# Sixteen transposes of a batch in one group, and an earlier carry, from the seventh batch on

## The chip, the cores and the metric

The kernel runs on one core of a Trainium2 chip. The core has five engines with an instruction queue each: TensorE (PE; PEld is its weight load, which overlaps the matmuls), VectorE (DVE), ScalarE (ACT), GpSimd (POOL), and SyncE (SP), which here only issues DMAs. An engine takes its queue in order, and the engines meet at semaphores. The metric is the device time of one execution in microseconds (us), lower is better; a time is the median of several runs.

## The reference

Sixteen batches of 512 tokens with 512 features each. One layer, in two halves:

```
# half 1: h = rmsnorm(layernorm(x)) * g_res @ W_in.T + b_in
#         p = rmsnorm(ctx)[..., :512] * g_init, scanned over the 512 patches: s[t] = a*s[t-1] + b*p[t]
#         plug = index of the patch of each token, from the running count of boundaries
x = x + s[plug] + h
# half 2 (z = layernorm(x)), z_prev = z shifted by one token
xr = mu_r * z + (1 - mu_r) * z_prev ;  xk = mu_k * z + (1 - mu_k) * z_prev
r  = sigmoid(xr @ W_r.T) ;  k = square(relu(xk @ W_k.T))
x  = x + r * (k @ W_v.T)
```

Everything is in float32. The four products (a: `W_in`, k: `W_k`, r: `W_r`, v: `W_v`) are each a 512x512 by 512x512 product per batch.

## The kernel before, in words

**Products.** Each operand of a product is split into a high and a low part, and a product is high*high + high*low + low*high. A product of a batch is four output tiles of 128x512; a tile is 12 matmuls of 128x512 (3 passes over 4 chunks). So a, k, r and v are 48 matmuls each per batch. In the text, "r tile 2" is the third tile of r; a "row product" is one tile of r or v, whose 128 rows are tokens.

**The stages of a batch b.**
- The context tiles `cx` (four of 128x1024) are loaded by SP; ACT squares them (`junk<-cx`), POOL takes the power (`sq`), DVE scales and chains them (`cx<-cx,sq,bc`, `cx<-cx,cx`: `scan_u`).
- The **carry** (`scan`, lines 744 to 780): three matmuls with a fixed matrix on the high and low parts `ch`, `cl` of the last context tile give `pc`; DVE adds it to the four tiles (`cx<-pc,cx`), SP writes them to a DRAM buffer (`dr<-cx`), and the next context tiles take their room.
- `x` is loaded, its statistics are taken, the bias is added by a POOL DMA (`x<-bc`), and the rows of the scan are added by four **gathers** (`x<-dr,plug`), indirect DMAs of POOL. The index `plug` is made for four batches at a time by small matmuls (`cp`) and DVE work.
- a: four tiles `pa`; `a_end` (`x<-pa,rs,x`, DVE) adds each to x and frees its PSUM tile. It needs the gathers of its rows.
- The second norm (`norm2`: `sb`, `r` on DVE and POOL, `y` on ACT), then the **transposes** (`transp`, lines 848 to 858): four 128x128 transposes for each of the four row tiles, sixteen in all, into the four tiles `tr`.
- `mix` (lines 860 to 878) makes from `tr` the operand `m` of k and of r: ACT (`pv<-tr`), DVE (`pv<-tr,small,pv`), ACT (high part, `m<-pv`), DVE or POOL (low part).
- k: four tiles `pk`; ACT takes relu, square and high part (`kr`, `kr<-kr`, `ka`), DVE or POOL the low part. r: `pr`, then ACT's sigmoid `sg`. v: `pw`, then DVE's `sg<-pw,sg`, and the sum into x, which is stored.

**The order.** A planner (`Plan`, lines 63 to 285) runs a model of the engines on the host while the kernel is built, and gives each engine a fixed order of "pieces" (the row "L300" of the profile is the helper that records every instruction, so groups are told apart by tile names). A piece has a cost, a due time, and a "late" time that is worked backwards from what needs it; `lead` is added to what a piece is held to need. The course of PE is laid out in slots: with i the batch in its second half, a of batch i+1 (as far as not done), k of batch i, then the row products of batch i in the order r0, r1, v0, r2, v1, r3, v2, v3, with the transposes of batch i+1 among them:

```
for k, (w, j) in enumerate((("r", 0), ("r", 1), ("v", 0), ("r", 2), ("v", 1), ("r", 3), ("v", 2), ("v", 3))):
    slot((w, i, j))
    if n1:
        for jj in TAT_OF.get(i, TAT).get(k, ()):
            slot(("t", i + 1, jj), 0.43)
```

`TAT = {0: (0, 1), 2: (2, 3)}` puts eight transposes behind the first row product and eight behind the third; `TAT_OF` has other places for the first batches. The transposes become free to run when the four `y` are there, so the second norm of batch i+1 ends before.

**PSUM tiles.** There are four PSUM tiles of the kind `ps` for pa, pk, pr, pw and pc, and four of the kind `tr`. The planner takes the lowest free one (line 230, `take[k] = (kind, sorted(free[kind])[used])`). In its order most products therefore alternate between two tiles: a product may start only when the engine behind the last product but one has read that one's result. A carry takes a third tile.

**SP.** Each load that takes a buffer also waits for a PE instruction (lines 1268 to 1272), so the loads keep to the planner's order.

Of the kernel before, what the change touches and what calls it, by code (L numbers as in the profile page):

```python
# [316 lines left out]
}  # L317
PASS = 0.935
PERIOD = lambda i: (("a", i + 1), ("k", i))
TAT = {0: (0, 1), 2: (2, 3)}  # L320
TAT_OF = {0: {0: (0, 1, 2, 3)}, 1: {0: (0, 1, 2, 3)}, 2: {0: (0, 1, 2, 3)}}
AHEAD = 20.0
EASE = 1.0
SKIP = 6.0
# [114 lines left out]
NWHOLE = 2  # L439
Y_DVE = (0, 1, 2, 3)  # L440
LEAD = 12.0
HI_DVE = False
U_DVE = True
LOADS = ["raw2"]
# [7 lines left out]
def block_kernel(  # L452
# [59 lines left out]
    def add(engines, fn, r=(), w=(), new=None, **kw):  # L512
        if isinstance(engines[0], str):
            engines = (engines,)
        kinds = {}
        for n, v in (new or {}).items():
            kinds[n], spec[n] = v[0], v[1:]
        kw["stage"] = stage
        if engines is LO and ONLY.get(stage) is not None:
            kw["port"] = (DVE, POOL)  # L520
            engines = (LO[ONLY[stage]],)
        elif engines is HI:
            kw["port"] = (DVE,) if HI_DVE else ()
        elif engines is LO:
            kw["port"] = (DVE, POOL)
        elif engines[0][0] == POOL and "moves" not in kw:
            kw["port"] = (POOL,)
        plan.add(engines, fn, r, w, kinds, **kw)

    def K(name, *parts):  # L530
        return [(name, p) for p in (parts or (0,))]
# [4 lines left out]
    PS = (("ps",), [P, D], F32)  # L536
    PST = (("ps", "tr"), [P, D], F32)
    TRP = (("tr", "ps"), [P, D], F32)
    TR = (("tr",), [P, D], F32)
    HI = ((ACT, 0.52), (DVE, 0.34)) if HI_DVE else ((ACT, 0.52),)  # L540
    LO = ((DVE, 0.61), (POOL, 1.26))
# [202 lines left out]
    def scan(b):  # L744
        def carry(e):
            e.matmul(S[f"pc{b}"], scan_m, S[f"cx{b}_{NJ - 1}"][:, :D], start=True, stop=True)

        if b < NWHOLE:
            add((PE, 1.12), carry, K(f"cx{b}_{NJ - 1}") + K("consts"), K(f"pc{b}"),
                new={f"pc{b}": PST if b == 0 else PS}, lead=LEAD if b > 1 else 0.0)  # L750
        else:
            last, hi, lo = f"cx{b}_{NJ - 1}", f"ch{b}", f"cl{b}"
            TMPR = (("tmp",), [P, D], F32R)
            if b == NWHOLE:
                add((ACT, 0.3), lambda e: e.copy(scan_hi, scan_m), K("consts"), K("scan_r", 0))
                add((DVE, 0.2), lambda e: e.tensor_tensor(scan_lo, scan_m, scan_hi.bitcast(F32), ALU.subtract),
                    K("consts") + K("scan_r", 0), K("scan_r", 1))
            add((ACT, 0.52), lambda e: e.copy(S[hi], S[last][:, :D]), K(last), K(hi), new={hi: TMPR})
            add(LO, lambda e: e.tensor_tensor(S[lo], S[last][:, :D], S[hi].bitcast(F32), ALU.subtract),
                K(last) + K(hi), K(lo), new={lo: TMPR})  # L760

            def carry3(e):
                for i, (w, m) in enumerate(((0, hi), (0, lo), (1, hi))):
                    e.matmul(S[f"pc{b}"], (scan_hi, scan_lo)[w], S[m], start=(i == 0), stop=(i == 2))

            add((PE, 0.72), carry3, K(hi) + K(lo) + K("scan_r", 0, 1), K(f"pc{b}"),
                new={f"pc{b}": PS}, lead=LEAD if b > 1 else 0.0)
        for j in J:
            n = f"cx{b}_{j}"
            add((DVE, 0.6),  # L770
                lambda e, n=n, j=j: e.scalar_tensor_tensor(
                    S[n][:, :D], S[f"pc{b}"], ADEC ** (j + 1), S[n][:, :D], ALU.mult, ALU.add),
                K(f"pc{b}"), K(n))

            def put(e, n=n, j=j):
                if f"dr{b}" not in S:
                    S[f"dr{b}"] = dpool.tile([T, D], F32, tag="dr", name=f"dr{b}")
                e.dma_start(S[f"dr{b}"].rearrange("(p j) d -> p j d", j=NJ)[:, j], S[n][:, :D])

            add((SP, 0.5), put, K(n), K(f"dr{b}", j), moves=0.73)  # L780
# [288 lines left out]
    def slot(key, cost=3 * PASS):  # L1069
        nonlocal t  # L1070
        due[key] = t
        t += cost
# [5 lines left out]
    for i in range(NB):  # L1078
# [5 lines left out]
# [5 lines that stand above are left out]
# [62 lines left out]
    def prepare_batch(b):  # L1151
# [34 lines left out]
        for j in J:  # L1186
            scan_u(b, j, one_go=b == 0 or U_DVE)
        scan(b)
        stage = ("stat1", b)
        for j in J:  # L1190
# [141 lines left out]
```

## Time and profile before

| What | us |
|---|---|
| median of 3 runs | 815.05 |
| lowest and highest run | 812.93, 817.34 |
| the profiled execution, device time | 813.32 |
| its span, from the first to the last instruction | 811.2 |
| PE busy in the span | 789.8 |
| DVE busy | 616.2 |
| ACT busy | 486.7 |
| POOL busy | 449.8 |

The granted clock of PE is 0.997 of full speed over the span. The chain that ended last is PE for 62% of the span, DVE for 12%, DMA for 9%, POOL for 6%, waits on nothing that the profile shows ("issue") 5%, ACT 4%. The three dearest issues of DMA: 64 loads of context tiles (512 KB each, 6.2 us to landing), 64 writes of the scan (256 KB, 3.4 us) and 14 bias additions (1024 KB, 8.1 us).

Busy time of PE is not read as work at its peak: matmuls are pipelined and the profile models their ends. The starts are better. In an undisturbed stretch a row of four 128x512 matmuls begins 0.93 us after the last such row, a tile of twelve takes 2.80 us, and eight transposes 0.79 us.

### The profile page before, as it was taken

The page shows a single profiled execution, that of the slowest core. Times are in us where ns is not written, and L with a number is a line of the kernel's source. Part 1 is how long each engine was busy: PE and PEld are TensorE (multiplying, and loading weights), DVE is VectorE, ACT ScalarE, POOL GpSimd, SP SyncE. Part 2 cuts the span into 40 slices and gives each one's busy share as a digit, 9 for nine tenths or more (in the row PEclk, how much of TensorE's full clock was granted, in tenths as well). Part 3 has the DMA queues.
Part 4 walks back from the last instruction along what each step waited for, and adds up shares of the span by engine and source line. Part 5 has one row for each costly group of instructions (what it writes and reads, how often), then busy time and mean ns, then how long its engine had stood idle before and what let it go on. Part 6 is the DMA issues. An engine that isn't in the chain of part 4 may idle for free.

```text
span 811.2 us, 11218 instructions
## 1 busy us (share of the span) xinstructions
PE 789.8 (97%) x3627; PEld 624.8 (77%) x3627; DVE 616.2 (76%) x1323; ACT 486.7 (60%) x950; POOL 449.8 (55%) x374
## 2 busy tenths in 40 slices
PE   7998999999999999999999999999999999999997
PEld 4776777877777887878787887888778787888885
DVE  6899799989789497686968779685876869784622
ACT  5937496555484566757455775646666564655640
POOL 2843676464675465763647566565665647571300
PEclk9999999999999999999999999999999999999999
DMA  9857486884784773847668392866559477350001
GB/s 321 271 96 263 101 235 175 280 216 131 157 232 131 181 232 74 241 166 198 156 140 242 74 268 107 218 198 184 135 130 246 136 173 216 66 141 2 27 27 52
DMA packets 52554, 134.69 MB, mean 166 GB/s; under 512 B 4752, under 2 KB 5264, under 8 KB 50576
## 3 DMA queue, kind: packets, MB, share of 16 engines
q1 hardware_dynamic: 35744, 102.39, 36.9%
q0 software_dynamic: 16608, 31.46, 23.0%
q8 instruction: 28, 0.46, 0.2%
q14 instruction: 30, 0.25, 0.1%
q10 hardware_dynamic: 144, 0.13, 0.0%
HBM read 85.73 MB, written 33.55 MB: 147 GB/s over the span
## 4 chain that ended last, share of the span: by engine, by line
PE 62%; DVE 12%; DMA 9%; POOL 6%; issue 5%; ACT 4%; SPq 0%; POOLq 0%; DVEq 0%; ACTq 0%
PE pk L300 19%; PE pr L300 15%; PE pw L300 14%; PE pa L300 11%; DMA x<-dr,plug 6%; DVE cx L300 4%; PE tr L300 3%; DVE pv L300 2%; DVE x L300 2%; POOL m L300 2%; DMA dr<-cx 2%; POOL x L300 2%; ACT pv L300 2%; PE pc L300 1%; ACT junk L300 1%
## 5 line engine op out<-in xcount | busy, mean ns | idle before, releaser
L300 POOL TENSOR_TENSOR m<-pv,m 128x512 fp32r<-128x512 f32 x79 | 117.1, 1492 | 54.6 <-ACT m L300 23.3
L300 PE MATMUL pr<-whr,m 128*128 128x512 f32 x512 | 141.7, 400 | 0.8 <-ACT sg L300 0.8
L300 PE MATMUL pa<-wha,xh 128*128 128x512 f32 x512 | 136.0, 400 | 5.6 <-DVE x L300 2.7
L300 POOL DMA_INDIRECT x<-dr,plug x64 | 109.8, 1715 | 55.8 <-DMA dr<-cx 16.8
L300 PE MATMUL pw<-whv,ka 128*128 128x512 f32 x512 | 138.9, 397 | 0.6 <-ACT sg L300 0.6
L300 PE MATMUL pk<-m,whk 128*128 128x512 f32 x512 | 134.4, 397 | 2.5 <-DVE x L300 2.1
L300 ACT ACTIVATE pv<-tr,om 128x384 f32<-128x384 f32 (+1 forms) x256 | 100.5, 488 | 57.7 <-PE tr L300 44.6
L300 PEld LDWEIGHTS pa<-wha,xh 128*128 128x128 f32 x512 | 94.8, 188 | 33.4 <-DVE x L300 7.3
L300 PEld LDWEIGHTS pk<-m,whk 128*128 128x128 f32 x512 | 95.2, 188 | 27.9 <-DVE x L300 2.9
L300 PEld LDWEIGHTS pw<-whv,ka 128*128 128x128 f32 x512 | 95.6, 188 | 24.1 <-ACT sg L300 1.8
L300 PEld LDWEIGHTS pr<-whr,m 128*128 128x128 f32 x512 | 94.0, 188 | 22.3 <-ACT sg L300 1.2
L300 DVE SCALAR_TENSOR_TENSOR pv<-tr,small,pv 128x511 f32<-128x511 f32 x128 | 95.0, 743 | 11.3 <-ACT pv L300 9.2
L300 ACT ACTIVATE y<-x,r 128x512 f32<-128x512 f32 x48 | 39.0, 816 | 97.3 <-DVE r L300 95.3
L300 DVE TENSOR_TENSOR sg<-pw,sg 128x512 f32<-128x512 f32 (+1 forms) x65 | 44.0, 678 | 55.6 <-PE pw L300 55.4
L300 POOL TENSOR_TENSOR xh<-raw,xh 128x512 fp32r<-128x512 f32 x48 | 64.4, 1348 | 39.1 <-ACT xh L300 22.6
L300 POOL TENSOR_TENSOR x<-x,sg 128x512 f32<-128x512 f32 x14 | 19.3, 1378 | 113.9 <-DVE sg L300 94.5
L300 ACT CAST m<-pv 128x512 fp32r<-128x512 f32 x128 | 73.2, 628 | 15.1 <-DVE pv L300 12.2
L300 ACT ACTIVATE junk<-cx 128x1024 bf16<-128x1024 f32 x64 | 67.9, 1061 | 12.3 <-DMA cx<-cx 11.6
L300 ACT ACTIVATE sg<-pr 128x512 f32<-128x512 f32 x64 | 38.1, 598 | 56.5 <-PE pr L300 47.3
L300 PE MATMUL pa<-wla,xh 128*128 128x512 f32 x256 | 70.4, 398 | 0.3 <-POOL wla L300 0.3
L300 PE MATMUL pw<-wlv,ka 128*128 128x512 f32 x256 | 70.7, 398 | 0.0
L300 PE MATMUL pr<-wlr,m 128*128 128x512 f32 x256 | 70.3, 396 | 0.0
(116 smaller groups left out, 1300.7 us busy)
## 6 DMA issues: line engine op xcount, KB each, us to landing
cx<-cx SPq DMA_DIRECT2D x64, 512.0 KB, 6.2
dr<-cx SPq DMA_DIRECT2D x64, 256.0 KB, 3.4
out<-x SPq DMA_DIRECT2D x31, 512.0 KB, 2.8
x<-x SPq DMA_DIRECT2D x15, 1024.0 KB, 4.9
x<-bc POOLq DMA_DIRECT2D x14, 1024.0 KB, 8.1
raw<-xT SPq DMA_DIRECT2D x26, 512.0 KB, 7.5
wsa<-winT SPq DMA_DIRECT2D x2, 512.0 KB, 4.4
x<-x SPq DMA_DIRECT2D x4, 256.0 KB, 7.0
```

Source lines behind the costliest of these rows:

```text
L300: r = self._tc.keep_in_program_order(op(*args, **kwargs))
```

## The change

Transposes: the default place is now behind slot 3 (r2, the fourth row product) and holds all sixteen. The old places are kept for the slots of i = 3 and 4 by name, so the default holds from i = 5, which is batch 6, the seventh, on. Carry: its `lead` is 15 in place of 12 from batch 6 on.

```diff
-TAT = {0: (0, 1), 2: (2, 3)}
-TAT_OF = {0: {0: (0, 1, 2, 3)}, 1: {0: (0, 1, 2, 3)}, 2: {0: (0, 1, 2, 3)}}
+TAT = {3: (0, 1, 2, 3)}
+TAT_OF = {0: {0: (0, 1, 2, 3)}, 1: {0: (0, 1, 2, 3)}, 2: {0: (0, 1, 2, 3)}, 3: {0: (0, 1), 2: (2, 3)}, 4: {0: (0, 1), 2: (2, 3)}}
...
 LEAD = 12.0
+LEAD_LATE = 15.0
+NLEAD = 6
...
             add((PE, 1.12), carry, K(f"cx{b}_{NJ - 1}") + K("consts"), K(f"pc{b}"),
-                new={f"pc{b}": PST if b == 0 else PS}, lead=LEAD if b > 1 else 0.0)
+                new={f"pc{b}": PST if b == 0 else PS}, lead=(LEAD if b < NLEAD else LEAD_LATE) if b > 1 else 0.0)
...
             add((PE, 0.72), carry3, K(hi) + K(lo) + K("scan_r", 0, 1), K(f"pc{b}"),
-                new={f"pc{b}": PS}, lead=LEAD if b > 1 else 0.0)
+                new={f"pc{b}": PS}, lead=(LEAD if b < NLEAD else LEAD_LATE) if b > 1 else 0.0)
```

No computation is added or taken away. Because the planner lays out all engines anew, every engine's order differs from about batch 5 on. In the built program the order of PE for a batch in the middle is (counts are matmuls or transposes; batch numbers in brackets):

```
before  a(10)x48  k(9)x48  r0(9)  t(10)x8  r1(9)x4  carry(11)x3  r1(9)x8  v0(9)  t(10)x8  r2 v1 r3 v2 v3
after   a(10)x16  carry(11)x3  a(10)x32  k(9)x48  r0 r1 v0 r2(9)  t(10)x16  v1 r3 v2 v3
```

Before, the carries of batches 8 and 12 stand in k(6) and k(10) behind 28 matmuls, and that of batch 6 among k(4) and r(4); after, that of batch 6 stands between a(5) and k(4). On the other engines the following moves with it: the squares `junk<-cx` of the next batch but one stand between the relus of k on ACT (before: among the row products), the DVE scan of the context stands behind the low parts of k (before: among `a_end` of a), the four carry additions `cx<-pc,cx` stand between `a_end` of tile 0 and of tile 2 (before: behind r0), and the gathers follow the bias on POOL without other work between, save those of batches 8 and 12, which keep their place among the low parts of `m`.

## The prediction

> **What bounds the kernel now.** I read the page's first two parts, then the waits of PE, then PE's timeline row by row, then those of DVE, POOL and ACT where PE stands still.
>
> ```profile
> PE 789.8 (97%) x3627; PEld 624.8 (77%) x3627; DVE 616.2 (76%) x1323; ACT 486.7 (60%) x950; POOL 449.8 (55%) x374
> PEclk9999999999999999999999999999999999999999
> ```
>
> PE is busy all through and its clock is not throttled, so what can be won is only the time in which PE's rows start late. In the timeline four matmuls of 128x512 start 0.93 us after the last four; what is more is lost:
>
> ```profile
> 489.64 1.09 PE L300 MATMUL pa<-wha,xh 128*128 128x512 f32 x4
> 490.90 1.20 PE L300 MATMUL pa<-wha,xh 128*128 128x512 f32 x4 [0.17 <-DVE x L300]
> 491.93 1.10 PE L300 MATMUL pa<-wla,xh 128*128 128x512 f32 x4
> 492.87 1.10 PE L300 MATMUL pa<-wha,xh 128*128 128x512 f32 x4
> 494.15 1.21 PE L300 MATMUL pa<-wha,xh 128*128 128x512 f32 x4 [0.18 <-DVE x L300]
> ...
> 594.60 1.09 PE L300 MATMUL pk<-m,whk 128*128 128x512 f32 x4
> 596.65 1.19 PE L300 MATMUL pk<-m,whk 128*128 128x512 f32 x4 [0.96 <-DVE x L300]
> 597.68 1.09 PE L300 MATMUL pk<-m,wlk 128*128 128x512 f32 x4
> ```
>
> 490.90 - 489.64 - 0.93 = 0.33, and the next row is 0.10 late too: 0.4 us a stall of this kind; the one at 596.65 is 1.12 + 0.10. Done for every start from 256.8 us (where the order of PE changes first) to the end, without the 0.08 us that follows each group of transposes, this gives **7.1 us**, by place:
> - tiles 2 and 3 of a, waiting for `a_end` (445.9, 490.9, 494.2, 638.7, 683.8, 687.0): 2.5
> - tile 1 of k, waiting for the last `a_end` (403.9 and 596.7, batches 8 and 12): 1.9
> - r1 behind the first transposes (319.9, 368.2, 560.2): 1.6
> - at carries 0.6; at v and `cp` 0.5.
>
> All are waits for a PSUM tile: with two tiles in turn, a product starts when the last but one has been read. Why `a_end` was late stands on DVE:
>
> ```profile
> 488.40 1.78 DVE L300 SCALAR_TENSOR_TENSOR cx<-cx,sq,bc 128x512 f32<-128x512 f32 x1 [0.94 <-POOL sq L300]
> 490.10 0.74 DVE L300 SCALAR_TENSOR_TENSOR x<-pa,rs,x 128x512 f32<-128x512 f32 x1
> ```
>
> The scan of the context, ahead of it in the queue, waited for POOL's power and then took 1.78 us where 0.75 is usual.
>
> **The change, part by part.** Below, E is the start of a (end of v3); tile n of a starts at 2.80 n, after the carry 0.70 later, so a's tiles 2 and 3 at 6.3 and 9.1, k's at 11.9, 14.7, 17.5, 20.3, and r0, r1 at 23.1, 25.9.
>
> *Transposes in one group.* Eight transposes take from 422.40 to 423.19 = 0.79 us and delay the next row by 0.08: 0.87. Sixteen take 15 x 0.109 + 0.03 + 0.08 = 1.74 = 2 x 0.87. **Worth nothing in itself.** They end 2.8 us later in the course; `mix` for k then has v1, r3, v2, v3 and a, 22.4 us and more, until k. In the last batch, which has no a behind it, it has 11.2 us: in the trace the four high parts of `m` are done at 764.2, 5.8 us after the transposes, the low parts at about 768.1, some 10, of which the second pass needs the last only at 13. Nothing lost, with 5 us to spare for the first pass.
>
> *Carry earlier.* By 96 matmuls and eight transposes for most batches: 96 x 0.2335 + 0.87 = 23.3 us, though the lead grows by 3. It has to wait for nothing new in the steady state: from one carry (609.74) to the low part for the next (649.28) went 39.5 us, and a period is 47.3. Its DMAs move with it: `dr` writes and three context loads now follow the load of x on SP instead of standing ahead of it by half a period; x is still loaded ahead of them. The gathers get half a period. For typical batches `a_end` no longer waits for data: the scan of the context and the power leave the stage. **2.5 us and 1.6 us (the r1 waits, where transposes no longer split r0 from r1) go.** What is late next:
>
> *(1) DVE in a.* Its queue, by the spacing of its rows: `sg` 0.72 from E+0.27, x 0.70, two `pv` 0.79 each, `a_end` 0 (0.77), `pv`, `m` 0.60, three `cx<-pc,cx` (2.48 for four, 0.62 each), `a_end` 1, done at 8.1 (needed 9.1); `cx`, two statistics (1.03 each), `a_end` 2, done at 11.5 (needed 11.9); statistics and one of the next x (0.93), `a_end` 3, done at 14.4 (needed 14.7). So margins of 1.0, 0.4, 0.3: no stall as it stands. The Trainium skill speaks against this part: the GPSIMD Engine Reference, section 1, Specifications, says that GpSimd shares its SBUF interface with VectorE, with contention when a DVE instruction has two SBUF inputs. Two of this queue do (x, `m`), while POOL makes low parts. The rows: x 1.07 mean against 0.69 free, `m` 0.86 against 0.68, together 0.56 above free; that would leave 0.2 us of stall. Had each of the two to sit out a whole POOL instruction (1.34, the row `xh<-raw,xh`), it would be 2.7 - 0.3 = 2.4 a period, over 20 us in all. I go by the mean rows; the margin is a near thing. **0.1 a period, 0.9; ends 0 and 0.5 a period (4.5).**
>
> *(2) ACT in k.* Rows 740.21 to 742.03: relu, square, high part take 1.82 us; a `junk<-cx` 1.06 to 1.17 more, now between them: 2.9 to 3.0 per tile where PE takes 2.80. ACT comes from `y` and `xh` (four of 0.73, four of 0.53), starting when `a_end` 2 and the statistics are through at 11.6; the relus end at 16.4, 20.1, 23.0, 25.9, needed at 17.5, 20.3, 23.1, 25.9. In the trace of before r1 had 0.87 us of transposes as cover and still waited three times. **0.15 a period, 1.35; ends 0 and 0.6 (5.4).**
>
> *(3) Gathers of batches 8 and 12* still wait for `plug`, which comes behind r3. The last starts on POOL 5.8 us after E (587.34 - 581.55) and is 8.5 us from its row to `a_end` (595.85); it stays there. k's tile 1 is now due 0.70 later: 1.9 becomes **0.4** (ends 0 and 1.9).
>
> *(4) Carry starts*, 0.06 for each of ten: **0.6**. *(5) The step into the new order:* carry 6 comes 15.7 us earlier, so context 7 is loaded earlier; in the trace the three loads are issued 4.3 to 8.3 us behind their carry and need about 6.2: ACT's squares, ahead of the relus of k(4), wait for them, about 2 us of which PE sees part; and the scan of context 6 stands ahead of `a_end` in a(5). **1.5** (ends 0 and 3). *Rest* 0.2.
>
> **Sum.** Gone 7.1; new 0.9 + 1.35 + 0.4 + 0.6 + 1.5 + 0.2 = 4.95. **2.15 us less**: 813.3 becomes 811.2 for an execution like the profiled one (811.2 span plus 2.1 around it), and since that one was 1.7 below the median of the runs shown, **812.9** for the median. No change by over 0.5% (4.1 us), about what a measurement can tell.
>
> **The rivals.**
> - *All stalls go* (the margins of 1 and 2 hold, the step costs nothing): left are 0.6 of the carries and about 0.7. 815.05 - 5.8 = **809.3**. For it: both queues come out just in time with usual rows. Against: there are no reserves, and DVE's two-input rows are slower than usual half of the time.
> - *ACT and DVE become the bound, slower*: in each period k on ACT costs 0.6 us and `a_end` 0.9 (both shared-port rows meeting a POOL instruction for half its length). 9 x 1.5 = 13.5 + 1.5 of the step + 1.0 of points 3 and 4 - 7.1 = +8.9: **824**. It decides from (7.1 + 4.1 - 2.7)/9 = 0.95 us a period. For it: PE has only two PSUM tiles in turn, so each delay of a reader is a stall. Against: the plan of before had DVE rows of 1.53 and 1.78 in a and lost just 0.45 each.
> - *PE waits for the carry itself*, in the midst of a: three context loads late on SP. The margin is 47.3 - 39.5 = 7.8 us; if loads and queues ate 9, 1.2 x 9 = 11 less 2.2: **824**. Against: nothing in the row of waits shows PE held by a carry's inputs for more than 0.2.
>
> **How the numbers follow.** Forecast 0.38, own range 810.9 to 817. All stalls go 0.32. Slower by ACT and DVE 0.23, by the carry 0.07. The range 808.4 to 822 leaves out half of the two slower cases (their times spread above and below 824) and little of the others. Faster 0.32, within 0.5% 0.38, slower 0.30.
>
> **What would show it.** PE busy at some 97% still; no wait of r1 behind transposes; in a, `DVE x` as releaser gone or under 0.2 us a period; the starts of k's tiles 2, 3 and r0, r1 with `ACT kr` as releaser, 0.1 to 0.3 late; the 596.65 stall down to about 0.4; context squares waiting for DMA only around batch 7. I am wrong if periods from k to k exceed 47.9 us on the mean, or if PE's waits name the carry's inputs.

## The result

| | us |
|---|---|
| kernel before, median of 11 runs on the same chip | 813.63 |
| changed kernel, median of 11 runs (819.05 to 821.97) | 820.11 |
| ratio, 95% interval | 1.0075 (1.0063 to 1.0087) |
| profiled execution of the changed kernel, span | 818.3 |

The changed kernel is slower by 0.75%, some 6 us; the forecast was 812.9, a gain of 2, with 810.9 to 817 as its own range. The page of the changed kernel, busy time and the granted clock by slices:

```profile
PE 793.1 (97%) x3627; PEld 629.5 (77%) x3627; DVE 603.9 (74%) x1331; ACT 485.1 (59%) x950; POOL 442.3 (54%) x366
PEclk8999999999999999999999999999999999999999
```

Nothing in it tells of a loss. PE is busy for 3.3 us more with the same work, and the span is 7.1 us longer. What tells is the course of PE in stretches, each from the last matmul of k of one batch to that of the next (worked out from the starts of PE's rows in both traces; 47.2 is a stretch in which nothing starts late, and 7 and 11 hold 0.6 us more in both kernels, the small matmuls of the index):

| stretch ends with k of batch | before | changed |
|---|---|---|
| 6 | 49.20 | 47.27 |
| **7** (a is that of batch 8) | 47.99 | **53.05** |
| 8, 9, 10 | 47.53, 48.30, 48.25 | 47.21, 47.22, 47.37 |
| **11** (a is that of batch 12) | 48.63 | **52.96** |
| 12, 13, 14 | 47.66, 48.33, 47.26 | 47.22, 47.22, 46.53 (no carry left) |

So the change does all that it could be hoped to do in seven stretches, and loses 5.1 and 4.3 us in two. From the end of k(5) to the end the sum is +2.9 us; the step into the new order, from the end of k(3) to that of k(5), is +1.2 (102.7 and 103.9), of which 0.7 are the three matmuls of the carry of batch 7, which now stand inside it and are missing in stretch 14; the other 3.0 of the 7.1 lie before the end of k(3), 2.8 of them before that of k(2), up to where all engines have the same orders and waits.

**The two stretches.** PE's timeline of the changed kernel around the first:

```profile
405.37 1.10 PE L300 MATMUL pk<-m,whk 128*128 128x512 f32 x4
409.71 1.20 PE L300 MATMUL pk<-m,whk 128*128 128x512 f32 x4 [3.24 <-DVE x L300]
410.74 1.74 PE L300 MATMUL pk<-m,wlk 128*128 128x512 f32 x4
412.28 2.98 PE L300 MATMUL pk<-m,whk 128*128 128x512 f32 x8
415.09 1.10 PE L300 MATMUL pk<-m,wlk 128*128 128x512 f32 x4
```

409.71 - 405.37 - 0.93 = 3.41 us in which k's tile 1 waits for the last `a_end`. Then rows of four take longer: 412.28 - 410.74 = 1.54 and (415.09 - 412.28) / 2 = 1.41 where 0.93 is usual. Eight matmuls start 0.43 us apart in place of 0.2335, and the view of stretches of time shows why (the third number from the end is the granted clock, ahead of the DMA share and GB/s):

```profile
405.00:409.00 4.00, 1.46 (x7) 0.84 (x5) 0.26 (x3) 1.12 (x3) 1.80 (x2) 1.00 1.03 322
411.00:412.00 1.00, 1.00 (x4) 0.81 (x3) 0.97 (x4) 1.00 (x3) 1.00 (x2) 0.50 0.92 283
412.00:413.00 1.00, 1.00 (x4) 0.81 (x3) 0.96 (x3) 0.97 (x2) 1.00 (x2) 0.50 0.44 164
415.00:416.00 1.00, 1.00 (x6) 0.79 (x5) 0.47 (x6) 0.97 (x4) 1.00 (x2) 1.00 0.00 0
```

The clock is halved for about 3.4 us behind the stall: another 1.5 us. In batch 12 it is 3.0 and 1.5. With the 0.1 us by which the row behind each stall is late too, the two places cost 5.0 and 4.6 us, 9.6 in all. (The expectations below were written with 5.4 each, 10.8 in all, which is 1.2 too much.)

`a_end` is late because its gather is. DVE's timeline of the changed kernel:

```profile
405.05 0.15 DVE L300 TENSOR_SCALAR r<-r 128x1 f32<-128x1 f32 x1
408.90 0.75 DVE L300 SCALAR_TENSOR_TENSOR x<-pa,rs,x 128x512 f32<-128x512 f32 x1 [3.70 <-DMA x<-dr,plug]
```

and POOL's, first of the kernel before, then of the changed one (a of batch 8 starts at E = 389.35 and at 391.62):

```profile
384.23 1.70 POOL L300 DMA_INDIRECT x<-dr,plug  x1 [3.76 <-DVE plug L300]
386.29 1.29 POOL L300 TENSOR_TENSOR m<-pv,m 128x512 fp32r<-128x512 f32 x1 [0.36 <-ACT m L300]
387.74 1.94 POOL L300 DMA_INDIRECT x<-dr,plug  x1 [0.16 <-issue]
389.09 1.93 POOL L300 TENSOR_TENSOR m<-pv,m 128x512 fp32r<-128x512 f32 x1
391.17 1.84 POOL L300 DMA_INDIRECT x<-dr,plug  x1 [0.16 <-issue]
392.44 1.90 POOL L300 TENSOR_TENSOR m<-pv,m 128x512 fp32r<-128x512 f32 x1
394.50 1.56 POOL L300 DMA_INDIRECT x<-dr,plug  x1 [0.16 <-issue]
```

```profile
389.58 1.70 POOL L300 DMA_INDIRECT x<-dr,plug  x1 [0.32 <-DVE plug L300]
391.57 1.87 POOL L300 DMA_INDIRECT x<-dr,plug  x1 [0.30 <-issue]
394.86 1.28 POOL L300 TENSOR_TENSOR m<-pv,m 128x512 fp32r<-128x512 f32 x1 [1.41 <-DVE x L300]
396.30 1.55 POOL L300 DMA_INDIRECT x<-dr,plug  x1 [0.15 <-issue]
397.28 1.90 POOL L300 TENSOR_TENSOR m<-pv,m 128x512 fp32r<-128x512 f32 x1
399.34 1.55 POOL L300 DMA_INDIRECT x<-dr,plug  x1 [0.16 <-issue]
```

The first gather moves from E-5.1 to E-2.0, since the index is ready at E-2.3 in place of E-5.4. Its first small matmuls stand 2.8 us later in PE's order (`cp<-ohj,oh`, at 378.46 = E-10.9 before and at 383.54 = E-8.1 after). The rest is on DVE, where its last rows stand behind later `pv` rows and beside rows of POOL (see the last section). Then POOL waits with the third gather behind a low part of `m` whose operand isn't there, because the transposes that it comes from are later: ACT is at its high part from 393.55 to 394.22. The last gather starts at E+7.7 in place of E+5.2, and takes 9.56 us to `a_end` in place of 8.62: 2.56 + 0.94 = 3.5 us later than before. The 0.70 us by which k is now due later cover only the 0.7 us that k's tile 1 had already waited before, so a stall of 3.4 us is left. The long way to `a_end` is the DMA's own: by the semaphores the gather has landed only 9.5 us behind its row, where the first three took 4.8 to 5.9 us, and the DMA engines are busy throughout (their share is 0.87 to 1.12 in each 2 us from 399 to 409).

### The profile page after: what moved, and what is told of

The parts are those of the page before. It is cut to its first block, busy times and chain, and to the rows that moved or that the text cites. A ratio compares the mean times of both kernels' runs of the same rounds, so it can differ in the third digit from the quotient of the medians.

```text
span 818.3 us, 11141 instructions
## 1 busy us (share of the span) xinstructions
PE 793.1 (97%) x3627; PEld 629.5 (77%) x3627; DVE 603.9 (74%) x1331; ACT 485.1 (59%) x950; POOL 442.3 (54%) x366
## 4 chain that ended last, share of the span: by engine, by line
PE 69%; DVE 13%; DMA 8%; issue 3%; POOL 3%; ACT 2%; SPq 0%; DVEq 0%; POOLq 0%; ACTq 0%
PE pk L300 18%; PE pr L300 17%; PE pw L300 17%; PE pa L300 14%; DMA x<-dr,plug 4%; DVE x L300 3%; PE tr L300 3%; DMA x<-x 3%; DVE cx L300 2%; DVE pv L300 2%; DVE sg L300 1%; PE pc L300 1%; DMA cx<-cx 1%; DMA out<-x 1%; POOL x L300 1%
## 5 line engine op out<-in xcount | busy, mean ns | idle before, releaser
L300 POOL TENSOR_TENSOR m<-pv,m 128x512 fp32r<-128x512 f32 x80 | 113.0, 1419 | 109.0 <-ACT m L300 50.4
L300 PE MATMUL pk<-m,whk 128*128 128x512 f32 x512 | 136.3, 401 | 6.8 <-DVE x L300 6.7
L300 PE MATMUL pr<-whr,m 128*128 128x512 f32 x512 | 138.6, 397 | 0.0
L300 POOL DMA_INDIRECT x<-dr,plug x64 | 112.7, 1760 | 46.7 <-issue 15.7
L300 PEld LDWEIGHTS pa<-wha,xh 128*128 128x128 f32 x512 | 96.8, 191 | 31.6 <-DVE x L300 3.2
L300 ACT CAST m<-pv 128x512 fp32r<-128x512 f32 x128 | 76.3, 643 | 41.1 <-DVE pv L300 36.1
L300 DVE TENSOR_TENSOR ka<-kr,ka 128x512 fp32r<-128x512 f32 x52 | 39.8, 764 | 75.0 <-ACT ka L300 74.9
L300 PE MATMUL pk<-m,wlk 128*128 128x512 f32 x256 | 71.3, 403 | 0.0
L300 POOL TENSOR_TENSOR r<-r,mhalf 128x1 f32<-128x1 f32 x64 | 40.0, 627 | 57.2 <-DVE r L300 47.0
```

Source lines behind the costliest of these rows:

```text
L300: r = self._tc.keep_in_program_order(op(*args, **kwargs))
```

## The experiments

For each kernel I give the stall and the gathers of batch 8 (batch 12 is alike). The ratio is to the kernel before in the same comparison.

**Carry alone**: the old `TAT` and `TAT_OF`, `LEAD_LATE = 15.0` kept.

> The old places of the transposes, the longer lead of the carry. Theory: the changed kernel is slow because in batches 8 and 12 the last gather is late on POOL, held by a late index (plug) and by low parts of m that the late transposes delay; here three gathers stand together ahead of those low parts, so the stall of k's tile 1 (3.4 and 3.0 us in the changed kernel) falls to 0.5 or less and the clock isn't lowered behind it: some 810 to 812 us, ratio to before 0.995 to 0.999. Rival, the DMAs of the earlier carry (four writes of the scan and a load of x) crowd the gathers: the gather still takes over 9 us to land and the stall stays over 2 us.

814.15 us, ratio 1.0002 (0.9987 to 1.0016). POOL's timeline (E = 392.93):

```profile
388.81 1.71 POOL L300 DMA_INDIRECT x<-dr,plug  x1 [0.31 <-DVE plug L300]
390.82 1.75 POOL L300 DMA_INDIRECT x<-dr,plug  x1 [0.30 <-issue]
392.87 1.55 POOL L300 DMA_INDIRECT x<-dr,plug  x1 [0.30 <-issue]
395.51 1.29 POOL L300 TENSOR_TENSOR m<-pv,m 128x512 fp32r<-128x512 f32 x1 [1.09 <-DVE x L300]
396.96 1.96 POOL L300 DMA_INDIRECT x<-dr,plug  x1 [0.16 <-issue]
```

Three gathers stand together, the last starts at E+4.0, and the stall is gone. From its row to `a_end` are 9.1 us, but `a_end` did not wait for the gather, which had landed after 5.2 us; so the crowding that the rival forecast is not there for a gather that starts this early, though the earlier carry's DMAs are. The time is no better all the same, and misses the 810 to 812 expected: from the end of k(5) on the trace wins 4.7 us, and loses 4.0 in the step into the new order (106.7 from k(3) to k(5)); 0.7 of both is the moved carry of batch 7. Most of the loss is at one product of r, which waits 2.2 us for ACT's `sg` at 272 us.

**Transposes alone**: `LEAD_LATE = 12.0`.

> The transposes in one group, the carry's lead as before. Theory of the late gather on POOL: two gathers, then low parts of m between the others as in the changed kernel, and no carry in a to give 0.70 us: the stall of k's tile 1 in batches 8 and 12 stays at 3 us or more, with the lowered clock behind it, 4.5 us and more each. Rival, crowding by the earlier carry's DMAs: these are no longer there, the last gather lands in 8.6 us or less and the stall is about 2.5 or less[...].

816.83 us, ratio 1.003 (1.0014 to 1.0047). The last gather is as late as expected, E+7.96, but I missed the rest: it is at `a_end` after 8.2 us (7.5 in batch 12), as the rival had it, and the plan gives k's tile 1 a third PSUM tile, since no carry in a holds one, so that only k's tile 2 waits, 0.16 us. The loss is in the batch after, in a of batches 9 and 13. PE's timeline:

```profile
441.20 1.10 PE L300 MATMUL pa<-wha,xh 128*128 128x512 f32 x4
444.62 2.08 PE L300 MATMUL pa<-wha,xh 128*128 128x512 f32 x4 [2.33 <-DVE x L300]
446.50 1.69 PE L300 MATMUL pa<-wla,xh 128*128 128x512 f32 x4
```

2.49 us and the halved clock behind it, 4.6 us in that stretch and 4.2 in the other. There the gathers wait for the scan's writes, 7.80 us of POOL's idle time, and a low part of `m` again stands among them:

```profile
431.23 2.03 POOL L300 DMA_INDIRECT x<-dr,plug  x1 [7.80 <-DMA dr<-cx]
```

So the late transposes make the last gather late with either lead, and which product pays for it depends on the lead; the earlier carry with the old places of the transposes has no such stall, but a dearer step into the new order.

**Index earlier**: the changed kernel, with two entries in `SHIFT`, the hand-set corrections of the late times.

```diff
+    ("plugs", 8): -20.0,
+    ("plugs", 12): -20.0,
```

> The changed kernel, with the index of batches 8 and 12 made some 20 us earlier, so that all four gathers stand ahead of the low parts of m. Theory of the late gather: both stalls of k's tile 1 go (5.4 us each with the slow clock), all periods from k to k come to 47.2 to 47.5 us: 820.1 - 10.8 = 809.3 us, 0.995 of before. Rival, that the stall has another cause (crowded DMAs, DVE): stalls over 2 us remain in the periods of batches 8 and 12, over 813 us.

812.03 us, ratio 0.9967 (0.9952 to 0.9982). The gathers start at E-19.7 to E-9.5, and no `a_end` waits for them. What is left are two waits of carries for `a_end` of tile 0 (`DVE x`), which is late by DVE's own queue, 1.0 and 0.6 us. This shows the cause: of the change itself nothing was undone, though the planner lays out the neighbourhood anew (six rows go from DVE to POOL). Of the 2.7 us by which it misses the expectation, 1.6 are these waits, and 1.2 had been counted too much in the two stalls.

**Two groups in the two batches**: the changed kernel, with `TAT_OF` entries 6 and 10 of `{0: (0, 1), 2: (2, 3)}`.

> The changed kernel, but in the two batches whose low parts of m meet the gathers of batches 8 and 12 the transposes are two groups of eight, as before. Theory of the late gather: with the transposes early the low parts of m are no longer late and three gathers stand together; the last gather starts about 2 us earlier on POOL and the stall falls below 1.5 us, without a lowered clock: 812 us or less. If the stall stays over 3 us, the place of the transposes has no part in it and the lateness of the index, or the DMAs, is the cause.

811.59 us, ratio 0.9961 (0.9950 to 0.9972). The index is ready at E-3.8, the last gather starts at E+4.9 and is at `a_end` after 7.3 us, having landed after 6.8: no stall. So the place of the transposes in two of ten batches was enough.

**PSUM tiles in turn.** The order of every engine stays the same to the instruction; of the free PSUM tiles of kind `ps` the planner takes the one that has been free the longest, not the lowest.

```diff
-        events, out = [], []
+        events, out, freed = [], [], {}
...
+                            freed[kind, s] = now
...
-                                take[k] = (kind, sorted(free[kind])[used])
+                                take[k] = (kind, sorted(free[kind], key=lambda s: freed.get((kind, s), 0.0) if kind == "ps" else s)[used])
```

On the changed kernel:

> The changed kernel with the order of every engine the same, but each product takes the PSUM tile that has been free the longest, so that four tiles go in turn in place of two. Theory: the gather is as late as before (about 7.8 us behind the start of a, landing at about 17), but k's tile 1 no longer needs the tile of a's last product; the next product that does is k's tile 3, due 20.3 us behind the start of a. Both stalls and the slow clock behind them go, 10.8 us: 809.3 us, 0.994 of before. Rival, that k's tile 1 waits for the last gather in another way than by its PSUM tile: the stall of 3.0 to 3.4 us stays, 820 us.

814.38 us, ratio 1.001 (0.9996 to 1.0025): some 5 us of the loss are back, but the rival was right in part. k's tile 1 no longer waits; v0 does. Timelines of ACT and PE:

```profile
408.92 0.82 ACT L301 ACTIVATE y<-x,r 128x512 f32<-128x512 f32 x1 [4.07 <-DVE r L301]
...
410.87 0.57 ACT L301 ACTIVATE kr<-pk 128x512 f32<-128x512 f32 x1
```

```profile
404.10 2.03 PE L301 MATMUL pk<-m,whk 128*128 128x512 f32 x8
...
419.04 0.86 PE L301 MATMUL pw<-whv,ka 128*128 128x512 f32 x3
422.73 0.68 PE L301 MATMUL pw<-whv,ka 128*128 128x512 f32 x1 [2.83 <-ACT ka L301]
```

k's tile 0 was done soon after 405, yet its relu starts at 410.87: ACT's queue has `y` of batch 8 ahead of it, whose `r` stands on DVE behind the `a_end` that waits for the gather. The delay runs through ACT's `ka` to v, where PE stops for 3.0 us, with the halved clock behind it. A late gather holds PE up through a queue if not through a tile. But this execution is the slowest of the twelve, 817.99 us, and from the end of k(5) on it is only 1.1 us shorter than that of the changed kernel. The times fall into two groups: six runs with a granted clock of 0.994 to 0.997 took 812.8 to 814.4 us, six with 0.989 to 0.991 took 814.4 to 818.0. A stretch of 3.41 us at half the clock takes 0.0021 off the mean, so the first six had one to three of them, where this trace has five; how long PE waited in them is not on record.

On the kernel before:

> The kernel before with the order of every engine the same and the PSUM tiles in turn. If all of the 7.1 us of stalls counted before are waits for a PSUM tile that another free one would spare, PE loses about 1 us from 256.8 us on, and 814.6 becomes 808.5 us, 0.993. Rival: what reads the tiles is late by its own work, and the stall only moves to the product that needs the operand (k's operands, v's): less than half of it goes, 811 us or more.

806.18 us, ratio 0.9914 (0.9881 to 0.9947), from 4 runs. Again, in more rounds:

> The kernel before with PSUM tiles in turn once more, in more rounds, since its first 4 runs spread over 4.9 us: if the gain is that of the 7.1 us of stalls, the ratio stays within 0.990 to 0.994 (806 to 809 us); if the first runs had a lucky start, 0.995 or more.

805.57 us, ratio 0.9895 (0.9872 to 0.9917). Its page:

```profile
PE 784.3 (98%) x3627; PEld 627.1 (78%) x3627; DVE 616.6 (77%) x1323; ACT 485.2 (60%) x950; POOL 451.9 (56%) x374
PEclk9999999999999999999999999999999999999999
```

From the end of k(5) on no start of PE is late by more than 0.15 us. That stretch is 6.9 us shorter than before, and the one from k(3) to k(5) 1.8. Three changed lines, which move no instruction, make the fastest kernel of this study, 1% under the kernel before and 1.8% under the changed one.

**Both cures.** Index earlier and tiles in turn:

> The changed kernel with the earlier index and the PSUM tiles in turn: both cures of the same stall. Theory: they don't add up, since either takes the whole of it away; what is left to win over the earlier index alone (812.0) is its two waits at the carries (1.0 and 0.6 us) and some of the start: 809 to 811 us. If they added up to another 5 us or more, each had cured a different thing.

810.55 us, ratio 0.9952 (0.9935 to 0.9968). Two groups and tiles in turn:

> The changed kernel with the transposes of the two batches in question in two groups, and the PSUM tiles in turn. Theory: as for the earlier index, no more than 2 us under the same kernel without the tiles in turn (811.6): what is left there are two waits of 0.7 us at the small matmul of the index, which no PSUM tile decides: 809.5 to 811.5 us.

811.66 us, ratio 0.9980 (0.9971 to 0.9989). As expected they don't add up (the second is 0.2 above its range): in both traces PE loses nothing more from the end of k(5) on, but for two waits of 0.7 us at the index in the second.

**The step into the new order.** Index earlier, tiles in turn, and `NLEAD = 7`:

> The changed kernel with tiles in turn and the earlier index, and its longer carry lead from batch 7 on in place of 6, so that the carry of batch 6 stays among the products k and r of batch 4, as before. Theory: what the step into the new order costs (the carry of batch 6 waits for its low part in the changed kernel, and the stretch from the end of k of batch 3 to that of k of batch 5 is 103.9 us against 102.7 before) goes, 1 to 4 us under the same kernel with NLEAD 6 (810.6): 807 to 809 us, level with the kernel before with tiles in turn. Rival, that the new order costs its entry wherever it begins: no gain, 810 us or more.

808.72 us, ratio 0.9925 (0.9902 to 0.9948). In the changed kernel the carry of batch 6, now between a(5) and k(4), waits for its low part:

```profile
259.51 0.39 PE L300 MATMUL pc<-ch,scan_hi 128*128 128x512 f32 x1
260.47 0.49 PE L300 MATMUL pc<-cl,scan_hi 128*128 128x512 f32 x1 [0.57 <-POOL cl L300]
```

Here it is back among k and r of batch 4, and the stretch from k(3) to k(5) is 101.8 us, where the same kernel with `NLEAD = 6` had 105.6, 1.5 of them by a halved clock behind its waits at this carry. From k(5) to the start of the last matmul both take 483.2 us, and the kernel before with tiles in turn 484.0, 0.7 of which is the carry of batch 7 that the others have ahead of k(5): the change's order, freed of its faults, and the old order with tiles in turn are worth the same there.

**What stays open.** The end of k(2), up to where no order differs, comes between 170.4 and 175.7 us in the twelve traces. Part of that is the clock: between 60 and 135 us it is never halved in three traces (ends 170.4 to 171.4), once in seven (171.4 to 174.3) and twice in two (both 175.7). Most of the rest arises at the waits of the transposes of batch 3, at about 130 us, 0.8 to 4.1 us long for the longest. Of the 2.8 us between the traces of before and changed, 1.1 follow a clock that is halved at 66 us in the changed kernel alone, and 1.9 arise at 128 to 130 us. The seven kernels with both parts of the change have the six latest of these ends, and some 2 us of the 6.5 between the medians of before and changed are not explained by the stretches behind it. Why the waits at 130 us differ in length I can't say, and whether it is chance is not settled. Nor did I separate what the carry's own DMAs add to a gather's landing. The last gather of batch 8 landed after 8.5 us before, 9.5 in the changed kernel, 8.1 with the late carry (transposes alone), and 5.2 and 6.8 where it starts at E+4.0 and E+4.9: when it starts seems to weigh more than whether the carry's DMAs are near.

## Why the prediction was wrong

**The step that failed is part (3).** It put the last gather of batches 8 and 12 at E+5.8, said "it stays there", and costed it at 0.4 us, 1.9 at the worst end. It was E+7.7 and E+8.1, 9.6 and 9.1 us to `a_end`, and 9.6 us of PE's time. I had read POOL's queue in the trace of before, where gathers alternate with low parts of `m`, and knew that the transposes moved 2.8 us later; I followed `mix` to k, where it has room, but not to POOL, where the gathers stand behind it. Nor did I ask what the index is queued behind, on PE and on DVE. And I priced no clock: 3.0 us of the 9.6 are the halved clock behind the stalls.

**Gone, 7.1 us: right.** No r1 waits behind transposes, no `DVE x` as releaser in a outside the two stretches. That these were waits for a PSUM tile is shown on the kernel before with tiles in turn, which loses them without any change of order.

**(1) and (2), 0.9 and 1.35: 0.** In the seven stretches no start is late by more than 0.11 us; the margins of 0.3 to 1.0 us held, and what ACT has between the relus cost PE nothing. The contention of DVE and POOL, for which the forecast cited the Trainium skill (GPSIMD Engine Reference, section 1, Specifications), cost the a stage nothing in these stretches; where it showed was at two small rows of the index (last section).

**(4), 0.6: hardly seen. (5), 1.5: measured 0.5** in the single traces (1.2 without the moved carry of batch 7 taken off). The longest wait, 0.7, is at the place that was named, the carry of batch 6; but what PE waits for there is the carry's own low part from POOL, not squares or scans behind context loads.

Without the two stalls the stretches and the step would have given 2.9 + 1.2 - 9.6 = -5.5 us, close to the -5.8 of the rival in which all stalls go. The two rivals on the slow side had their 824 from ACT and DVE, and from the carry's own inputs, which is not what happened; that 820 lies near them, and inside the wide range of 808.4 to 822, is chance.

## What to carry to other kernels

A step that is moved late carries all that is queued behind its products, on every engine: look for the queue in which its consumers alternate with something that another stage waits for, here gathers among low parts on POOL. A stall that appears only in every fourth batch is found by cutting the trace into periods; the page's averages did not show it. And before an order is changed to win back waits for a buffer, look at which buffer is handed out: taking the one that has been free the longest won 1%, more than any form of the reordering that was tried.

## What the runs showed of the hardware

PE's clock was halved for 3.41 us behind waits of 3.4, 3.0 and 2.5 us, at a cost of about 1.5 us each. The Trainium skill, TensorE: Matmul & The Clock Gate, Part 1, says that the gate opens after about 3.4 us of sustained work, which agrees with how long the clock stays halved, and that it closes after an idle window of the same length; here 2.5 us were enough.

The length of the wait is not all that counts. A wait of 2.2 us (2.15 to 2.29) at 66 us stands in all twelve traces; a halved clock followed in seven, that of the changed kernel among them, and not in five, that of before among them. In every trace the changes of the granted clock are whole multiples of 3.413 us apart. Cut at these points, the twelve traces have 16 stretches of 3.413 us between 40 and 800 us in which PE is busy for less than 43% (by the profile, which models the ends of matmuls), and the clock is halved in the next stretch after every one of them; it is after three of the six with 43 to 51%, and after none above. So a wait of some 2 us costs its own length, or about 1.5 us more, by how much of it falls into one such stretch.

A tiny row on DVE waited out a whole row of POOL. The last row of the index (128x16), first in the kernel before, then in the changed one with POOL's row beside it:

```profile
383.77 0.17 DVE L300 CAST plug<-pf 128x16 int32<-128x16 f32 x1
```

```profile
387.98 1.28 POOL L300 TENSOR_TENSOR m<-pv,m 128x512 fp32r<-128x512 f32 x1
388.08 1.21 DVE L300 CAST plug<-pf 128x16 int32<-128x16 f32 x1
```

It ends 0.03 us after POOL's row. The row ahead of it (`pf<-pf`, 128x16) does the same, 0.57 us in place of 0.17. In the twelve traces these two rows stand 48 times for batches 8 and 12: the 28 that started while POOL had no arithmetic running took 0.17 or 0.18 us, and the other 20 ended 0.03 to 0.04 us after the row that POOL was at.
